# Scan layer of a two-layer block: operand offsets for GpSimd, VectorE's order over two units, and one PSUM bank moved

## The chip, the cores and the metric

The kernel runs on one core of a Trainium2 chip. A core has five engines that run side by side, each with its own in-order queue: TensorE (PE; its weight loads are listed as PEld), VectorE (DVE), ScalarE (ACT), GpSimd (POOL) and SyncE (SP), which here issues the DMAs. On-chip memory is SBUF, with 128 partitions, and PSUM, into which TensorE writes, used here as 8 banks of 512 float32 a partition. The metric is the device time of one execution in microseconds. Before the change, three runs gave a median of 8442.23 (8434.59 to 8457.52).

## The reference

The input is a 2 x 96 x 96 x 96 image batch (batch, channels, height, width). Layer 0 normalises over channels and goes through a 2-D selective scan; layer 1 is an attention layer; each is followed by a feed-forward block in a small float format. Only layer 0's scan changes. Cut to that:

```python
def selective_scan(u, delta, A, Bm, Cm, Dv):        # u: (windows, K=4, 192, L=36)
    def step(hst, inputs):
        ut, dt, bt, ct = inputs
        dA = jnp.exp(dt[..., None] * A)              # A: 16 states a channel
        hst = hst * dA + (dt * ut)[..., None] * bt[:, :, None, :]
        y = jnp.einsum('bkdn,bkn->bkd', hst, ct)
        return (hst, y)
    ...
    return jnp.moveaxis(ys, 0, -1) + Dv[None, :, :, None] * u
```

The image is cut into windows of 6 x 6 tokens, so a sequence has 36 tokens. Four directions are scanned: by rows, by columns, and both backwards. Ahead of the scan stand an input projection to 192 channels, a 3 x 3 convolution with GELU that gives an offset for every pixel, and a bilinear sampling at those offsets; behind it stand a layer norm, a gate and an output projection.

## The kernel before

**Staging.** Layer 0 works in 32 stripes (two images, 16 rows of windows); a stripe has T = 576 tokens. Three functions describe a stripe's work. `_l0_front` normalises, projects, convolves (`convolve`, L567), samples bilinearly on GpSimd (`sample`, L625 to L631) and makes the scan's inputs: the step sizes `dl` and the products `du` (the GpSimd lines L759 to L762 in `steps`), which go out to DRAM, and the B and C rows. `_l0_scan` runs the selective scan. `_l0_back` normalises, gates (L937) and projects its result and does the feed-forward block. While one stripe is scanned, the next one's front and the last one's back run between its instructions.

**The scan.** For each half of the channels, order and direction (`_l0_section`), four quarters `i` handle 4 of the 16 states each, and each quarter has two units `c` of 288 tokens: 64 units a stripe, 2048 in all. A partition is one (channel, state) pair, three channel blocks lie side by side, so an instruction works on 128 x 864 elements. A unit does this:

- `spread` (TensorE, L1056): copies the B row of its states to all partitions of the PSUM tile `bp`, a matmul with a 0/1 matrix;
- `product` (VectorE, L1060): multiplies `dur` with it and writes the product over all of `bp`, the last block first, so the B row is read before it is overwritten;
- `scan` (VectorE, L1076): runs h = h * dA + product along the tokens and writes `h` to SBUF;
- `times_c` (GpSimd, L1081): multiplies `h` in place by the C row, `cre`;
- `states` (TensorE, L1093): sums over states by matmul with `fold` into the PSUM tile `y`.

`decay` (ScalarE, L1041) makes `dA`, the exponentials, for both units of a quarter. SyncE loads `cre` for every quarter, `dlr` and `dur` for every section. There are six `h` buffers, two `dA`, two `bp`. The first unit's product also carries waits by hand (the `wait` call) for the decays of its quarter and for GpSimd and TensorE to be done with the `h` buffers that both units will use.

**PSUM.** `bp` has 2 buffers of 2 banks, `y` one bank, and the remaining 3 banks are the tag `p` (`P.np`), from which the front and the back take every matmul result: `pc` (convolution), `pb`, `pd`, `pt` (scan inputs), `yc`, `fxc` and so on.

**Offsets in SBUF.** A tile made with `skip=n` gets n unused elements (4 bytes each) at its front; `_place` cuts the view. Tiles are allocated at multiples of 32 bytes. `h` has a skip of 2, 4, 8 or 1 by quarter, with `lead=8` so that all have one size; `cre` has none. `dl`, `du`, `r`, `x1`, `x2`, `zs` and `fr` have different skips too.

**The order.** Nothing is issued directly. Each operation goes as an `_Op` with an engine, an estimated cost, the tiles it reads and writes, and a due time, to a planner (`_Plan`). `order()` is a list scheduler: it keeps a clock for each engine, adds a lag (`LAG`, by the engine that must wait) when the result comes from another engine, and picks the operation that can start first, with ties going to the earlier due time. Tiles take their buffers in the plan's order. The engines then run their instructions in exactly that order (`_in_order`); real waits are semaphores between them. A tile from `held` has no buffer and serves only to order operations. The unit's due times are `t0`, one `tau` = 3.4 us a unit.

Of the kernel before, what the change touches and what calls it, by code (L numbers as in the profile page):

```python
# [9 lines left out]
F32 = mybir.dt.float32  # L10
# [16 lines left out]
C = 96  # L27
HW = 96
# [62 lines left out]
class _Op:  # L91
    def __init__(self, eng, cost, run, due, tab):
        self.eng, self.cost, self.run, self.due, self.tab = eng, cost, run, due, tab
        self.deps, self.tiles, self.start, self.end = set(), [], None, None
        self.left, self.then, self.ready = 0, [], 0.0

SAME = 0.06  # L100
LAG = {"pe": 0.5, "dve": 1.5, "act": 0.6, "pool": 1.0, "sp": 1.5}


class _Plan:
# [6 lines left out]

    def tile(self, pool, shape, tag, bufs=1, dtype=F32, name=None, skip=None, lead=0):
        t = _Tile(self, pool, tag, bufs, shape, dtype, name or tag)
        t.skip, t.lead = skip, lead or skip
        return t
# [30 lines left out]
    def order(self):  # L146
# [13 lines left out]
        while len(out) < len(self.ops):  # L160
# [42 lines left out]
            for p in o.then:  # L203
                p.left -= 1
                p.ready = max(p.ready, o.end + (SAME if p.eng == o.eng else LAG[p.eng]))
                if not p.left:
                    ready[p.eng].append(p)
# [23 lines left out]
def _place(t, tag):  # L231

    if t.skip is None:
        return t.pool.tile(t.shape, t.dtype, tag=tag, name=t.name, bufs=1)
    n = math.prod(t.shape[1:])
    flat = t.pool.tile([t.shape[0], n + t.lead], t.dtype, tag=tag, name=t.name, bufs=1)
    v, d = flat[:, t.skip : t.skip + n], t.shape[1:]
    names = [f"d{j}" for j in range(len(d))]
    if len(d) == 1:
        return v  # L240
    return v.rearrange(f"p ({' '.join(names)}) -> p {' '.join(names)}", **dict(zip(names[1:], d[1:])))
# [200 lines left out]
def _cost(eng, cols):  # L442

    if eng == "pe":
        return 0.00175 * cols
    if eng == "act":
        return 0.2 + 0.0009 * cols
    if eng == "pool":
        return 0.1 + 0.00235 * cols
    return 0.08 + 0.00115 * cols  # L450
# [9 lines left out]
def _l0_front(k, P, S, f, x, b, s, at):  # L460
# [22 lines left out]
    def pool(cols, run, r, w):  # L483
        S.op("pool", _cost("pool", cols), run, r, w)


    xt, xin = temp([C, 8, HW], "xt"), S.tile(P.front, [C, 2, 8, HW + 2], "xin", 1)
    if lo > r0:
# [9 lines left out]
    )  # L498
    pool(8, lambda: nc.gpsimd.memset(xin.ap[:, :, :, 0 : HW + 2 : HW + 1], 0.0), (), (xin,))
    rows = lambda t, c: t.ap[:, 4 * c : 4 * c + 4, :].rearrange("p r w -> p (r w)")  # L500
# [26 lines left out]
    def project(half, c):  # L527
# [4 lines left out]
        act(N4, lambda: nc.scalar.copy(  # L532
            xin.ap[:, half, 4 * c : 4 * c + 4, 1 : HW + 1],
            pi.ap[:C, :N4].rearrange("p (r w) -> p r w", w=HW)), (pi,), ((xin, (half, c)),))
# [7 lines left out]

    zs = f.zs = S.tile(P.hand, [C, 2, T], "zs", 2, skip=12)

# [17 lines left out]
    def convolve(oh, c):  # L562
        pc = ps("pc")

        def part(ih, tap):
# [3 lines left out]
                k.w_c1[:, ih, tap, oh * C : (oh + 1) * C],  # L569
                xin.ap[:, ih, 3 * c + dy : 3 * c + dy + 3, dx : dx + HW],  # L570
                start=(ih == 0 and tap == 0),
# [16 lines left out]

    fr = temp([C, 2, WIN, HW], "fr", 5)

# [24 lines left out]
    xs1 = S.tile(P.front, [C, 2, T], "xs1", 1)  # L615
    dif, top, bot = temp([C, 2, 7, HW], "dif"), temp([C, 2, WIN, HW], "top", 2), temp([C, 2, WIN, HW], "bot")
    g = nc.gpsimd
    tt = g.tensor_tensor

    def sample(half):  # L620
        v = lambda: xin.ap[:, half, 1:8, 1 : HW + 1]
        fy, fx = lambda: fr.ap[:, 0], lambda: fr.ap[:, 1]
        d, tp, bt = (lambda u=u: u.ap[:, half] for u in (dif, top, bot))
        D, TP, BT = (dif, half), (top, half), (bot, half)
        pool(672, lambda: tt(d(), xin.ap[:, half, 1:8, 2 : HW + 2], v(), ALU.subtract), (xin,), (D,))  # L625
        pool(T, lambda: tt(tp(), d()[:, 0:6], fx(), ALU.mult), (D, (fr, 1)), (TP,))
# [35 lines left out]
    def order_of(o, xs):  # L662
# [50 lines left out]

        x1, x2 = row("x1", 1, skip=14), row("x2", 1, skip=9)

# [14 lines left out]
        def steps(m):  # L730
# [3 lines left out]
            u = x2 if m == 2 else x1  # L734
            e, du, r, w = (row(name, 2, skip=n) for name, n in (("e", 0), ("du", 1), ("r", 2), ("dl", 6)))
            for c in range(2):
# [271 lines left out]
def _l0_section(k, P, S, f, first, o, h, kk, py, at, tau):  # L1008
# [41 lines left out]
    def unit(u, i, c, cre, dA, t0):  # L1050
        toks = slice(c * H2, (c + 1) * H2)
        bp = S.tile(P.ps, [128, 1024], "bp", 2)
        ht = S.tile(P.rep, [128, NBL, H2], "h", P.nh, skip=(2, 4, 8, 1)[i], lead=8)

        def spread():
            nc.tensor.matmul(  # L1056
                bp.ap[:, :H2], k.selb[:, kk, i, :], f.bc[o].ap[:, toks], start=True, stop=True)

        def product():
            nc.vector.tensor_tensor(  # L1060
                bp.ap[:, : NBL * H2].rearrange("p (b n) -> p b n", b=NBL)[:, ::-1],
                dur.ap[:, ::-1, toks],
                bp.ap[:, :H2].unsqueeze(1).to_broadcast([128, NBL, H2]), ALU.mult)
            if c == 0:
                free = u + 1 - P.nh
                wait([("act", u), ("pool", free), ("pe", free)])

        S.op("pe", 0.3, spread, (f.bc[o],), (bp,), due=t0 - P.early["pe"] * tau)
        S.op("dve", 1.03, product, (dur,), (bp,), due=t0 - P.early["dve"] * tau)

        def scan():
            hv, dv = (v.rearrange("p b n -> p (b n)") for v in (ht.ap, dA.ap[:, c]))
            bv = bp.ap[:, : NBL * H2]
            if kk:
                hv, dv, bv = hv[:, ::-1], dv[:, ::-1], bv[:, ::-1]
            nc.vector.tensor_tensor_scan(hv, dv, bv, 0.0, ALU.mult, ALU.add)  # L1076

        S.op("dve", 2.0, scan, (dA, bp), (ht,), due=t0 + (1.35 - P.early["dve"]) * tau)

        def times_c():  # L1080
            nc.gpsimd.tensor_tensor(  # L1081
                ht.ap, ht.ap, cre.ap[:, toks].unsqueeze(1).to_broadcast([128, NBL, H2]), ALU.mult)
            P.issued["pool", u] = latest()

        S.op("pool", 2.06, times_c, (cre,), (ht,), due=t0 + (2.3 - P.early["pool"]) * tau)

        def states():
            end = o == 1 and kk == 1 and i == NQ - 1

            def part(dst, v, stop):  # L1090
                if o:
                    v = v.rearrange("p (w j i) -> p w i j", i=WIN, j=WIN)
                nc.tensor.matmul(dst, k.fold, v, start=False, stop=stop)  # L1093

            for blk in range(NBL):
                dst = py.ap[CB * blk : CB * blk + CB]
                n = HEAD - H2 if c else H2
                part(dst[:, c * H2 : c * H2 + n], ht.ap[:, blk, :n], end and c == 1)
            if c:
                for blk in range(NBL):  # L1100
                    part(_tail(py, blk), ht.ap[:, blk, n:], end and blk == NBL - 1)
            P.issued["pe", u] = latest()

        S.op("pe", 1.0, states, (ht,), (py,), due=t0 + (3.5 - P.early["pe"]) * tau)

# [4 lines left out]
def _layer0(k, tc, a, x, x2d):  # L1110
# [3 lines left out]
    with ExitStack() as st:  # L1114
# [12 lines left out]
        P.early = {"pe": 60, "act": 60, "dve": -30, "pool": 0, "sp": 8}  # L1127
        P.np, P.ng, P.nda, P.nh = 3, 5, 2, 6
        start = len(nc.cur_bb.bb.instructions)
        S, tau = _Plan(k), 3.4  # L1130
        stripes = [(b, s) for b in range(NB) for s in range(NW)]
        F = [Ctx() for _ in stripes]
# [834 lines left out]
```

## Time and profile before

| what | value |
|---|---|
| median of 3 runs | 8442.23 us |
| the profiled execution | 8449.37 us, span 8447.6 us |
| TensorE matmul busy in the span | 7320.6 us (87%) |
| VectorE busy | 7806.9 us (92%) |
| ScalarE busy | 6339.6 us (75%) |
| GpSimd busy | 5742.1 us (68%) |
| granted TensorE clock, mean | 0.907 |
| HBM traffic | 111 GB/s over the span |

The profile is of one execution. "Busy" is time in which at least one instruction of an engine ran; matmuls are pipelined, so a busy TensorE is not one at its peak. A line of the groups reads: source line, engine, operation, output <- inputs, shape, count | busy us, mean ns of one | idle time of the engine just before them and what ended most of it. A float32 matmul appears as two records. A line of a timeline reads: start, duration, engine, source line, operation, output <- inputs, shape, count; several equal ones in a row are merged into one.

### The profile page before, as it was taken

How to read it: one execution, taken by the hardware profiler on the slowest of the kernel's cores; microseconds unless marked ns; L12 is line 12 of the kernel's file. 1: busy time of each engine (PE TensorE's matmuls, PEld its weight loads, DVE VectorE, ACT ScalarE, POOL GpSimd, SP SyncE). 2: the span in 40 equal slices, each digit the busy share in tenths (PEclk: the TensorE clock that was granted, in tenths of full speed). 3: DMA queues.
4: the chain of work that ended last, by engine and by line, in shares of the span. 5: the costliest groups of instructions: out<-in, count | busy, mean ns of one | idle time of the engine just before them, and what ended most of it. 6: DMA issues, size and time to landing. Idle time of an engine off the chain costs nothing. (4 is left out here: it accounts for less than half of the span.)

```text
span 8447.6 us, 118902 instructions
## 1 busy us (share of the span) xinstructions
PE 7320.6 (87%) x43653; PEld 3406.4 (40%) x43653; DVE 7806.9 (92%) x5398; ACT 6339.6 (75%) x10688; POOL 5742.1 (68%) x3835
## 2 busy tenths in 40 slices
PE   7888888888888888888888888888857999989998
PEld 4444444444444444444444444444423223542245
DVE  3999999999999999999999999999996998959988
ACT  5777777777777777787777877787745886778867
POOL 4999989888889889999988999999873000110001
PEclk8898989999899889999989998999867999989999
DMA  2444444444444444444444444444442000110001
GB/s 89 142 153 152 152 154 150 149 153 146 148 151 149 149 148 153 155 151 150 155 152 147 149 153 150 152 154 155 147 135 63 3 2 14 36 48 3 2 22 33
DMA packets 339992, 985.62 MB, mean 117 GB/s; under 512 B 50152, under 2 KB 51872, under 8 KB 339104
## 3 DMA queue, kind: packets, MB, share of 16 engines
q1 hardware_dynamic: 337488, 977.74, 37.1%
q8 instruction: 347, 5.69, 0.3%
q14 instruction: 253, 2.07, 0.1%
q10 hardware_dynamic: 1904, 0.12, 0.0%
HBM read 797.19 MB, written 139.25 MB: 111 GB/s over the span
## 5 line engine op out<-in xcount | busy, mean ns | idle before, releaser
L1081 POOL TENSOR_TENSOR h<-h,cre 128x864 f32<-128x864 f32 x2048 | 3965.5, 1947 | 616.1 <-DVE h L1076 357.4
L1076 DVE TENSOR_TENSOR_SCAN h<-dA,bp 128x864 f32<-128x864 f32 x2048 | 3996.8, 1953 | 105.4 <-PE y L1093 27.2
L1041 ACT ACTIVATE dA<-dlr,A 128x576 f32<-128x576 f32 x3072 | 2156.5, 765 | 886.1 <-DVE h L1076 828.6
L1060 DVE TENSOR_TENSOR bp<-dur,bp 128x864 f32<-128x864 f32 x2048 | 2133.6, 1043 | 132.9 <-PE bp L1056 51.1
L1093 PE MATMUL y<-h,fold 128*32 128x288 f32 (+2 forms) x18432 | 1841.2, 446 | 154.4 <-POOL h L1081 152.6
L567 PE MATMUL pc<-xin,off 96*96 96x288 f32 x4608 | 1328.1, 420 | 0.0
L1056 PE MATMUL bp<-bt,selb 128*128 128x288 bf16 x2048 | 644.1, 316 | 700.4 <-DVE h L1076 683.7
L1429 ACT ACTIVATE pr<-sc 128x960 f32<-128x960 f32 (+1 forms) x1080 | 954.0, 937 | 202.8 <-PE sc L1425 182.5
L1093 PEld LDWEIGHTS y<-h,fold 128*32 128x32 f32 x18432 | 755.0, 117 | 857.6 <-issue 376.1
L1509 DVE TENSOR_TENSOR sums<-sums,pr 128x3840 f32<-128x3840 f32 (+1 forms) x240 | 959.0, 3996 | 56.9 <-ACT pr L1429 34.7
L567 PEld LDWEIGHTS pc<-xin,off 96*96 96x96 f32 x4608 | 705.2, 165 | 497.8 <-issue 247.2
L1601 POOL MEMSET vch<- 96x32 f32 x16 | 2.4, 152 | 1304.6 <-DVE dist L1463 1213.4
L1056 PEld LDWEIGHTS <-selb 128*128 128x128 bf16 x2048 | 201.5, 99 | 1455.9 <-DVE h L1076 1231.0
L1425 PE MATMUL sc<-qH,kH 32*128 32x480 f32 (+1 forms) x3240 | 627.2, 602 | 10.4 <-DMA q<-qH 5.6
L1425 PE MATMUL sc<-q,kH 32*128 32x480 f32 (+1 forms) x1080 | 564.7, 602 | 0.0
L1491 PE MATMUL av<-pr,vT 128*32 128x480 f32 (+1 forms) x4320 | 533.4, 564 | 3.6 <-ACT av L1516 3.5
L1682 DVE SCALAR_TENSOR_TENSOR acc<-vch,lepe_w,acc 96x1152 f32<-96x1152 f32 x320 | 469.0, 1466 | 7.9
L1425 PEld LDWEIGHTS sc<-qH,kH 32*128 32x128 f32 x3240 | 219.0, 184 | 419.7 <-issue 223.8
L883 POOL TENSOR_TENSOR x<-x,fy 96x576 f32<-96x576 f32 x32 | 53.3, 1664 | 479.1 <-ACT fy L882 415.1
L740 PE MATMUL pt<-xd,w_dt 96*128 96x288 f32 x768 | 304.1, 492 | 21.7 <-ACT xin L532 10.6
L761 POOL TENSOR_TENSOR dl<-dl,r 128x576 f32<-128x576 f32 x192 | 270.9, 1411 | 9.1 <-ACT dl L758 4.1
L762 POOL TENSOR_TENSOR du<-dl,x 128x576 f32<-128x576 f32 x192 | 271.7, 1415 | 6.6
(270 smaller groups left out, 9902.7 us busy)
## 6 DMA issues: line engine op xcount, KB each, us to landing
cre<-c_d SPq DMA_DIRECT2D x1024, 288.0 KB
dur<-du_d SPq DMA_DIRECT2D x256, 864.0 KB
dlr<-dl_d SPq DMA_DIRECT2D x256, 864.0 KB
x<-xs SPq DMA_DIRECT2D x512, 72.0 KB
du_d<-du SPq DMA_DIRECT2D x128, 288.0 KB
dl_d<-dl SPq DMA_DIRECT2D x128, 288.0 KB
du_d<-du SPq DMA_DIRECT2D x128, 144.0 KB
dl_d<-dl SPq DMA_DIRECT2D x128, 144.0 KB
```

The source lines that it names most:

```text
L567: pe(H2, lambda: nc.tensor.matmul(pc.ap[:C, :H2], k.w_c1[:, ih, tap, oh * C : (oh + 1) * C], xin.ap[:, ih, 3 * c + dy : 3 * c + dy + 3, dx ...
L1041: nc.scalar.activation(dA.ap[:, :, blk, :], dlr.ap[:, blk, :].rearrange("p (c n) -> p c n", c=2), AF.Exp, scale=k.A[:, i, kg, h, blk : blk ...
L1056: nc.tensor.matmul(bp.ap[:, :H2], k.selb[:, kk, i, :], f.bc[o].ap[:, toks], start=True, stop=True)
L1060: nc.vector.tensor_tensor(bp.ap[:, : NBL * H2].rearrange("p (b n) -> p b n", b=NBL)[:, ::-1], dur.ap[:, ::-1, toks], bp.ap[:, :H2].unsquee ...
L1076: nc.vector.tensor_tensor_scan(hv, dv, bv, 0.0, ALU.mult, ALU.add)
L1081: nc.gpsimd.tensor_tensor(ht.ap, ht.ap, cre.ap[:, toks].unsqueeze(1).to_broadcast([128, NBL, H2]), ALU.mult)
L1093: nc.tensor.matmul(dst, k.fold, v, start=False, stop=stop)
L1425: nc.tensor.matmul(two[to // 2][:, to % 2, :n], kH[rows, k0 : k0 + 128], q, start=True, stop=True)
L1429: nc.scalar.activation(pr[:, 2 * i : 2 * i + 2, :n], two[i][:, :, :n], AF.Exp, scale=HD**-0.5)
L1491: nc.tensor.matmul((main if s < HEADS else other)[s * HD : (s + 1) * HD, :n], vT[:, blk, hd, :], pr[:, place(s, p), :n], start=at == 0, st ...
L1509: nc.vector.tensor_tensor(both, both, pr[:, :, :, :n], ALU.add)
L1682: S.op("dve", 1.43, lambda: nc.vector.scalar_tensor_tensor(acc.ap, src(), W.lw[:, t : t + 1], acc.ap, ALU.mult, ALU.add), (vch,), (acc,))
```

## The change

Four edits of the scan's schedule and layout; the arithmetic is the same.

1. **Offsets.** `h` always has a skip of 2 elements, 8 bytes against `cre`; `du`, `r`, `x1`, `x2`, `zs` and `fr` get 2, `dl` gets 0, `top` 1. `xin` gets rows of 100 elements instead of 98 with the image at element 2. The parameter `lead` goes. The planner's cost of a GpSimd operation becomes 0.2 + 0.00177 us a column, and 1.75 for `times_c`.
2. **VectorE's order.** The two units of a quarter go as product, product, scan, scan. This is done with the held tile `turn`, which every product and scan writes, and by putting off the first unit's `rest()` until the second unit's product is planned.
3. **Banks.** The second unit's spread writes into a tile `B` of its own (one bank), and its product reads from there; the tag `p` gets 2 banks instead of 3.
4. **Lag.** For operations behind a spread the planner assumes 0.6 us on VectorE instead of 1.5 (`SOON`), since an `_Op` now carries its own lags.

```diff
+SOON = {"dve": 0.6}
...
-                p.ready = max(p.ready, o.end + (SAME if p.eng == o.eng else LAG[p.eng]))
+                p.ready = max(p.ready, o.end + (SAME if p.eng == o.eng else o.lag[p.eng]))
...
     if eng == "pool":
-        return 0.1 + 0.00235 * cols
+        return 0.2 + 0.00177 * cols
...
-    xt, xin = temp([C, 8, HW], "xt"), S.tile(P.front, [C, 2, 8, HW + 2], "xin", 1)
+    xt, xin = temp([C, 8, HW], "xt"), S.tile(P.front, [C, 2, 8, HW + 4], "xin", 1)
...
-    zs = f.zs = S.tile(P.hand, [C, 2, T], "zs", 2, skip=12)
+    zs = f.zs = S.tile(P.hand, [C, 2, T], "zs", 2, skip=2)
...
-    fr = temp([C, 2, WIN, HW], "fr", 5)
+    fr = temp([C, 2, WIN, HW], "fr", 2)
...
-        pool(672, lambda: tt(d(), xin.ap[:, half, 1:8, 2 : HW + 2], v(), ALU.subtract), (xin,), (D,))
+        pool(672, lambda: tt(d(), xin.ap[:, half, 1:8, 3 : HW + 3], v(), ALU.subtract), (xin,), (D,))
...
-        x1, x2 = row("x1", 1, skip=14), row("x2", 1, skip=9)
+        x1, x2 = row("x1", 1, skip=2), row("x2", 1, skip=2)
...
-            e, du, r, w = (row(name, 2, skip=n) for name, n in (("e", 0), ("du", 1), ("r", 2), ("dl", 6)))
+            e, du, r, w = (row(name, 2, skip=n) for name, n in (("e", 0), ("du", 2), ("r", 2), ("dl", 0)))
...
         bp = S.tile(P.ps, [128, 1024], "bp", 2)
-        ht = S.tile(P.rep, [128, NBL, H2], "h", P.nh, skip=(2, 4, 8, 1)[i], lead=8)
+        pB = S.tile(P.ps, [128, 512], "B", 1) if c else bp
+        ht = S.tile(P.rep, [128, NBL, H2], "h", P.nh, skip=2)
...
-                bp.ap[:, :H2].unsqueeze(1).to_broadcast([128, NBL, H2]), ALU.mult)
+                pB.ap[:, :H2].unsqueeze(1).to_broadcast([128, NBL, H2]), ALU.mult)
...
-        S.op("pe", 0.3, spread, (f.bc[o],), (bp,), due=t0 - P.early["pe"] * tau)
-        S.op("dve", 1.03, product, (dur,), (bp,), due=t0 - P.early["dve"] * tau)
+        S.op("pe", 0.3, spread, (f.bc[o],), (pB,), due=t0 - P.early["pe"] * tau).lag = SOON
+        S.op("dve", 1.0, product, (dur, pB) if c else (dur,), (bp, P.turn), due=t0 - P.early["dve"] * tau)
+
+        def rest():
+            def scan():
...
+            S.op("dve", 2.0, scan, (dA, bp), (ht, P.turn), due=t0 + (1.35 - P.early["dve"]) * tau)
...
-        S.op("pool", 2.06, times_c, (cre,), (ht,), due=t0 + (2.3 - P.early["pool"]) * tau)
+            S.op("pool", 1.75, times_c, (cre,), (ht,), due=t0 + (2.3 - P.early["pool"]) * tau)
...
+        if c == 0:
+            P.behind = rest
+        else:
+            P.behind()
+            rest()
...
-        P.np, P.ng, P.nda, P.nh = 3, 5, 2, 6
+        P.np, P.ng, P.nda, P.nh = 2, 5, 2, 6
...
+        P.turn, P.behind = S.held(k.ident, "turn"), None
```

## The prediction

> **What bounds the kernel now.** I read the busy times and the windows first, then the groups of instructions, then the timelines of single engines. The chain of waits follows the end of the run, which is layer 1, and says nothing of the part that changes. Two windows cut the run where the scan of layer 0 begins and ends (the columns are the window, its length, then busy time and instructions of PE, PEld, DVE, ACT, POOL, the granted clock, DMA share and GB/s):
>
> ```profile
> 145.00:6392.00 6247.00, 5292.92 (x31360) 2567.91 (x31358) 6051.30 (x4280) 4734.32 (x8163) 5575.11 (x3611) 0.89 0.48 149
> 6392.00:8447.00 2055.00, 1925.38 (x11979) 780.42 (x11976) 1739.72 (x1023) 1540.08 (x2401) 126.91 (x174) 0.96 0.08 21
> ```
>
> In the first, VectorE is busy 97% of the time, GpSimd 89%, TensorE 85%. So layer 0 runs at VectorE's pace, 6247 us for 32 stripes of 64 units, and the 2055 us of layer 1 stay. The groups say what VectorE does there and what it waits for:
>
> ```profile
> L1081 POOL TENSOR_TENSOR h<-h,cre 128x864 f32<-128x864 f32 x2048 | 3965.5, 1947 | 616.1 <-DVE h L1076 357.4
> L1076 DVE TENSOR_TENSOR_SCAN h<-dA,bp 128x864 f32<-128x864 f32 x2048 | 3996.8, 1953 | 105.4 <-PE y L1093 27.2
> ...
> L1060 DVE TENSOR_TENSOR bp<-dur,bp 128x864 f32<-128x864 f32 x2048 | 2133.6, 1043 | 132.9 <-PE bp L1056 51.1
> ```
>
> One product and one scan a unit, and little idle time: 132.9 us before products, of which 45.4 is the first load, and 105.4 before scans. The waits of this stretch name PE (51.1 and 28.8 before products, 27.2 before scans) and a handful of microseconds from others: some 124 us of stalls that a schedule could remove.
>
> **The order of VectorE.** VectorE's timeline (start, duration) has both orders in it, the old one nearly everywhere and the new one by chance a few dozen times:
>
> ```profile
> 4138.67 1.04 DVE L1060 TENSOR_TENSOR bp<-dur,bp 128x864 f32<-128x864 f32 x1
> 4139.74 1.95 DVE L1076 TENSOR_TENSOR_SCAN h<-dA,bp 128x864 f32<-128x864 f32 x1
> 4141.61 1.04 DVE L1060 TENSOR_TENSOR bp<-dur,bp 128x864 f32<-128x864 f32 x1
> 4142.69 1.95 DVE L1076 TENSOR_TENSOR_SCAN h<-dA,bp 128x864 f32<-128x864 f32 x1
> 4144.56 1.04 DVE L1060 TENSOR_TENSOR bp<-dur,bp 128x864 f32<-128x864 f32 x1
> ...
> 4150.45 2.00 DVE L1060 TENSOR_TENSOR bp<-dur,bp 128x864 f32<-128x864 f32 x2
> 4152.36 3.79 DVE L1076 TENSOR_TENSOR_SCAN h<-dA,bp 128x864 f32<-128x864 f32 x2
> 4156.07 1.04 DVE L1060 TENSOR_TENSOR bp<-dur,bp 128x864 f32<-128x864 f32 x1
> ```
>
> A scan that reads the product just before it starts 1.07 us after it, 0.03 after its end; an instruction that does not need its neighbour starts about 0.08 before the neighbour ends. Two units in the old order take 4144.56 - 4138.67 = 5.89 us; two in the new order 4156.07 - 4150.45 = 5.62 (others in the trace 5.64). So a pair gains 0.25 to 0.27. There are 1024 pairs, and in the records 1957 of the 2048 scans follow their product directly (elsewhere another instruction lies between and the gap is gone already): 0.956 x 1024 = 979 pairs, times 0.25 to 0.27, is 245 to 264 us. I take **-245**.
>
> The Trainium skill speaks against this: "VectorE: DVE Perf Modes", section "The DRAIN you can't avoid", measures a chain of copies as equally long with and without semaphores and says that such chaining gains nothing. By that sentence the reorder would be worth 0; the rows above disagree for a dependent pair, and the measured rows decide.
>
> **GpSimd's pairs.** GpSimd's timeline shows two prices for one shape:
>
> ```profile
> 3025.31 1.73 POOL L1081 TENSOR_TENSOR h<-h,cre 128x864 f32<-128x864 f32 x1
> ...
> 3028.52 1.71 POOL L1081 TENSOR_TENSOR h<-h,cre 128x864 f32<-128x864 f32 x1 [0.33 <-DVE h L1076]
> 3030.19 1.41 POOL L761 TENSOR_TENSOR dl<-dl,r 128x576 f32<-128x576 f32 x1
> 3031.91 2.03 POOL L1081 TENSOR_TENSOR h<-h,cre 128x864 f32<-128x864 f32 x1 [0.31 <-PE pt L740]
> ```
>
> Counted through the 2048 records, the first two of every eight take 1.71 us and the other six 2.02 (a quarter of one and three of the other give 1.945, the group's mean 1947). The first two are quarter i = 0, whose h lies 2 elements (8 bytes) off; the others lie 4, 8 and 1 off. The change puts all at 2: 1536 x 0.31 = 476 us less. `dl<-dl,r` and `du<-dl,x` (1.41 us, 4, 8 or 3 apart) should come to the 1.21 of `e<-e,du` and `r<-r,e`: 384 x 0.2 = 77. `Y<-Y,zs` adds 64 x 0.2 = 13. Together some 565 of GpSimd's 5575 us. The front's sampling (1.20 and 1.30) has no slow row to gain from; if `dif`, whose two reads stay one element apart, went to the slow rate, 64 x 0.2 = 13 us would come back.
>
> The skill's "GPSIMD Engine Reference", section 2.1, calls about 2.5 cycles an element a floor for two inputs; as an estimate that is 1.80 us for 864 elements at its 1.2 GHz, a gain of 0.22 a call instead of 0.31. The quarter at 1.71 is below it.
>
> None of this is on the path by itself: products and scans last 1.04 and 1.95 beside a busy or an idle GpSimd alike. Its worth is in the stalls. The stalls behind `y` (28.8 + 27.2) are TensorE's fold matmuls waiting for GpSimd, with the next spread behind them in TensorE's queue; part of the 51.1 is the same. Bounds 0 and -124; I take **-50**, near the 56 that the rows name. Without this cover the gain on VectorE would have met a GpSimd that needs 5575/32 = 174 us a stripe.
>
> **The spread and its bank.** The first unit's spread still writes into bp and needs the scan of the same slot. In the old order a scan and a product (2.95 us) lie between that scan's end and the product that needs the spread; in the new one a single scan, 1.87. The second unit's spread has a bank of its own, free as soon as the second product is done. But that product now stands ahead of the first scan: if its spread is late, both scans wait behind it. In the trace a free TensorE starts a spread 0.06 us after the scan's end and needs 0.30. Of 1024 first spreads, 101 start over 1.4 us after it, 85 us beyond in sum. So 0 to +85; since a stall once paid lets TensorE catch up, and part of the lateness is GpSimd's, I take **+30**.
>
> **TensorE's density.** Where the convolution runs, TensorE is full already:
>
> ```profile
> 2223.00:2295.00 72.00, 69.06 (x394) 33.80 (x386) 70.08 (x52) 53.64 (x85) 59.94 (x39) 0.89 0.48 149
> ```
>
> If VectorE is 4% faster (245 of 6247), these 72 us should be 69.1, all of which TensorE needs. If VectorE gets none of its gain here, 32 x 2.9 = +93; if the plan spreads the convolution, 0. I take **+45**.
>
> **Two banks for p.** I paired each p tile's first matmul with its last read: 11,997 us of holding in layer 0, 375 a stripe, 1.9 of 3 banks on average. Two banks over a stripe of 187 us offer 374. That would not do if holds were fixed, but much of them is queueing: `pb` is held 13.9 us for a few matmuls and copies of under 1 us, `pc` 19.2 for 36 matmul records of 0.29 (1328.1/4608), 10.4 of TensorE. Holds that shrink by a tenth suffice. From 0 to the third rival's price; I take **+10**.
>
> **What costs nothing.** No DMA is added, and SyncE's queue keeps its 1 load a quarter. The decays for quarter q+2 still wait for the second scan of q and have a pair's time, 5.62 in place of 5.89, for 3 x 0.70 us of ScalarE; without that slack each pair would lose what they overrun. The new costs and the shorter lag only move instructions. Layer 1 is planned with the new GpSimd cost, but has 126.91 us of GpSimd in 2055: 0 within 10.
>
> **Sum**: -245 - 50 + 30 + 45 + 10 = -210. The profiled execution took 8449.37 (span 8447.6), 7 above the median 8442.23, so 8239 there and **8232** against the median.
>
> **Rivals.**
> 1. The wait moves to the first spread: TensorE's queue is late for the shorter window. For it: 101 late spreads, the full stretch above, a granted clock of 0.70 in some windows. Against: the spread starts 0.06 us after its scan in most pairs. Price: +85 and +93 in full, nothing from GpSimd: 8442 - 245 + 178 = 8375.
> 2. Everything fits: stalls vanish with GpSimd's slack and pairs take 5.62: 8442 - 264 - 80 = 8098.
> 3. Slower: the two p banks set the pace. For it: 1.9 banks held on average. If holds stay at 375 us and each of 64 tiles a stripe loses 0.3 us at the hand-over between engines, a stripe takes (375 + 19)/2 = 197 us in place of 195.2, and the front's late work holds up spreads by the 85 above: 8442 + 58 + 85 = 8585. It decides once a stripe's holds pass 2 x 195 = 390 us.
> 4. The change does not do what it says: the next instruction still waits in the new order, as when two products in the trace were followed by a scan 2.5 us later. With some of GpSimd's relief against the tighter spread, 8440.
>
> **How the numbers follow.** Forecast 0.60, rival 1 0.16, rival 2 0.08, rival 3 0.12, rival 4 0.04. The forecast's own range is 8130 to 8340; reaching half into rivals 1 and 2 gives 8110 to 8430 with two tenths outside. This kernel's runs tell 0.3% (25 us) from no change: faster 0.83, same 0.04, slower 0.13.
>
> **What would show it.** The change's scans start about 0.96 after the second product and 1.86 after the first scan; `h<-h,cre` has a mean near 1715; `dl` and `du` near 1210; GpSimd's share in layer 0 falls to about 0.83; `PE y` vanishes among VectorE's waits while `PE bp` grows. It is wrong if products sit idle behind `PE bp` for over 200 us, or if matmuls of the front wait for ScalarE to empty a p bank.

## The result, and the profile after

The changed kernel takes **9131.14 us** (median of 4 runs, 9121.35 to 9136.23) against 8445.17 for the kernel before beside it: 1.0811 times as long, interval 1.0794 to 1.0828. It is slower by 686 us, where 210 less was forecast. The profiled execution took 9136.23 us, its span is 9134.4.

The same two windows as before, around the scan of layer 0 and after it (window, length, then busy time and instructions of PE, PEld, DVE, ACT, POOL, granted clock, DMA share, GB/s):

```profile
145.70:7082.20 6936.50, 5653.79 (x31374) 2760.20 (x31372) 5866.08 (x4280) 4831.68 (x8248) 5036.81 (x3609) 0.83 0.42 135
7082.20:9134.00 2051.80, 1926.66 (x11982) 780.48 (x11982) 1740.07 (x1023) 1541.09 (x2401) 127.29 (x175) 0.96 0.08 21
```

Layer 1 is as it was (2051.8 for 2055). Layer 0 went from 6247 to 6936.5 us, though VectorE's work in it shrank from 6051 to 5866 and GpSimd's from 5575 to 5037. VectorE is busy 85% of the time where it was busy 97%: the bound has become a wait. The groups name it:

```profile
L1079 DVE TENSOR_TENSOR_SCAN h<-dA,bp 128x864 f32<-128x864 f32 x2048 | 3884.6, 1937 | 926.8 <-PE y L1096 917.0
L1084 POOL TENSOR_TENSOR h<-h,cre 128x864 f32<-128x864 f32 x2048 | 3485.8, 1715 | 1796.7 <-DVE h L1079 858.3
...
L1062 DVE TENSOR_TENSOR bp<-dur,bp 128x864 f32<-128x864 f32 x1024 | 1068.4, 1043 | 150.2 <-ACT dA L1042 54.1
```

The scans sat idle 926.8 us, where they had been idle for 105.4; 917.0 of it ended when TensorE's matmuls into `y` (L1096, called the fold below) had read an `h` buffer. VectorE's stalls of over 0.1 us within layer 0, added up from its records, are 1070 us, before 132: 938 more. Layer 0 grew by 689, so the pairs did give back 249 us, about the 245 that the new order was to bring. The change did both things at once, and the loss is nearly four times the gain.

**Where the wait stands.** It comes at the same units of every stripe: in the mean of the 32 stripes 12.5 us in units 0 to 7, 5.8 in units 8 to 15 and 12.7 in units 32 to 39, of 33.4 in all. VectorE's timeline at the start of one stripe (start, duration; the bracket is the idle time before and its releaser):

```profile
2316.81 3.79 DVE L1079 TENSOR_TENSOR_SCAN h<-dA,bp 128x864 f32<-128x864 f32 x2
2320.52 1.04 DVE L1062 TENSOR_TENSOR bp<-dur,bp 128x864 f32<-128x864 f32 x1
2321.47 1.05 DVE L1062 TENSOR_TENSOR bp<-dur,B 128x864 f32<-128x864 f32 x1
2335.83 3.80 DVE L1079 TENSOR_TENSOR_SCAN h<-dA,bp 128x864 f32<-128x864 f32 x2 [13.32 <-PE y L1096]
2339.55 1.04 DVE L1062 TENSOR_TENSOR bp<-dur,bp 128x864 f32<-128x864 f32 x1
```

These are units 6 and 7 of the stripe: the six `h` buffers are full, and none comes free before TensorE has folded one. TensorE's timeline of the same time shows why it doesn't:

```profile
2322.70 4.06 PE L568 MATMUL pc<-xin,off 96*96 96x288 f32 x16
2326.60 0.28 PE L856 MATMUL fph<-fxq,f0w1q 96*128 96x288 fp8e5 x1
2326.73 3.08 PE L568 MATMUL pc<-xin,off 96*96 96x288 f32 x12
2329.65 0.28 PE L856 MATMUL fph<-fxq,f0w1q 96*128 96x288 fp8e5 x1
2329.77 3.57 PE L568 MATMUL pc<-xin,off 96*96 96x288 f32 x14
2333.18 1.13 PE L597 MATMUL po<-t,w_off 96*96 96x288 f32 x4
2334.24 0.61 PE L983 MATMUL y<-xs,w_D 96*32 96x504 f32 x1
...
2335.11 1.28 PE L1096 MATMUL y<-h,fold 128*32 128x288 f32 x22
```

`direct` (L983) opens the `y` bank of the new half and must come before every fold. It stands in TensorE's fixed order behind the next stripe's convolution (L568), which at this point should have been done. The windows of eight units of the stripe from 2303.66 show that, counting the convolution alone (window, length, busy time and instructions of PE and PEld, granted clock, DMA share, GB/s):

```profile
2303.66:2339.55 35.89, 25.71 (x99) 15.37 (x98) 1.00 0.37 111
2339.55:2368.72 29.17, 0.00 (x0) 0.00 (x0) 0.66 0.36 111
2368.72:2391.85 23.13, 0.00 (x0) 0.00 (x0) 0.99 0.53 169
2391.85:2414.34 22.49, 0.00 (x0) 0.00 (x0) 0.91 0.38 122
2414.34:2454.11 39.77, 0.00 (x0) 0.00 (x0) 0.66 0.48 147
2454.11:2479.24 25.13, 0.00 (x0) 0.00 (x0) 0.58 0.31 102
2479.24:2503.12 23.88, 0.00 (x0) 0.00 (x0) 0.80 0.43 151
2503.12:2525.96 22.84, 13.45 (x46) 6.79 (x46) 1.00 0.47 153
```

The fourth window, 22.49 us for four pairs, is the pace that the order was to bring (5.62 a pair). The convolution begins in the last eight units of the stripe and spills into the first eight of the next, where TensorE is full and VectorE waits. In the kernel before it lay in the last 24 units and was over in time. The last three windows of a stripe there, cut and counted in the same way:

```profile
2238.88:2264.14 25.26, 17.90 (x51) 9.20 (x52) 0.80 0.47 145
2264.14:2287.71 23.57, 14.19 (x51) 7.14 (x49) 1.00 0.50 154
2287.71:2311.28 23.57, 12.31 (x45) 6.69 (x44) 1.00 0.41 125
```

So the front is late, and the front's matmul results all go through the p banks.

**What holds the p banks.** Pairing each p tile's first matmul with its last read, as for the prediction: a stripe held banks for some 375 us before and some 363 now; three banks were all in use about 30% of the time before, and the two are both in use about 70% of the time now. One holder stands out. The back needs its `yc` tiles two at a time: the copy out of the first overwrites `Y`, which the second one's matmul still reads, so the first keeps its bank until the second has one too. TensorE's timeline of one stripe, two `yc` tiles of a pair and the tiles between:

```profile
2360.29 1.28 PE L909 MATMUL yc<-Y,less_mean 96*96 96x288 f32 x2 [0.82 <-ACT xs L648]
2361.36 1.17 PE L909 MATMUL yc<-Y,minus_mean 96*96 96x288 f32 x2
2364.39 1.28 PE L640 MATMUL px<-top,ident 96*96 96x288 f32 x2
...
2408.39 0.73 PE L909 MATMUL yc<-Y,minus_mean 96*96 96x288 f32 x2 [0.86 <-ACT r L747]
2408.95 0.65 PE L909 MATMUL yc<-Y,less_mean 96*96 96x288 f32 x2
```

From 2360.3 to 2413.6 one of two banks is held by half a pair, and everything between goes through the other one. The mean hold of a `yc` tile is 17.5 us (longest 56.7), before 6.1 (longest some 17).

### The profile page after: what moved, and what is told of

Same layout as the page of the kernel before. It is cut to its first block, busy times and chain, and to the rows that moved or that the text cites. A ratio compares the mean times of both kernels' runs of the same rounds, so it can differ in the third digit from the quotient of the medians.

```text
span 9134.4 us, 119246 instructions
## 1 busy us (share of the span) xinstructions
PE 7685.6 (84%) x43653; PEld 3596.2 (39%) x43653; DVE 7622.0 (83%) x5398; ACT 6434.5 (70%) x10768; POOL 5203.6 (57%) x3835
## 5 line engine op out<-in xcount | busy, mean ns | idle before, releaser
L1079 DVE TENSOR_TENSOR_SCAN h<-dA,bp 128x864 f32<-128x864 f32 x2048 | 3884.6, 1937 | 926.8 <-PE y L1096 917.0
L1084 POOL TENSOR_TENSOR h<-h,cre 128x864 f32<-128x864 f32 x2048 | 3485.8, 1715 | 1796.7 <-DVE h L1079 858.3
L1096 PE MATMUL y<-h,fold 128*32 128x288 f32 (+2 forms) x18432 | 1838.3, 455 | 292.0 <-POOL h L1084 287.8
L568 PE MATMUL pc<-xin,off 96*96 96x288 f32 x4608 | 1253.4, 409 | 13.5 <-ACT fh L859 7.0
L1096 PEld LDWEIGHTS y<-h,fold 128*32 128x32 f32 x18432 | 793.1, 121 | 1157.0 <-POOL h L1084 698.6
L1062 DVE TENSOR_TENSOR bp<-dur,bp 128x864 f32<-128x864 f32 x1024 | 1068.4, 1043 | 150.2 <-ACT dA L1042 54.1
L1062 DVE TENSOR_TENSOR bp<-dur,B 128x864 f32<-128x864 f32 x1024 | 1076.0, 1051 | 0.0
L568 PEld LDWEIGHTS pc<-xin,off 96*96 96x96 f32 x4608 | 711.2, 162 | 404.3 <-issue 62.7
L1058 PE MATMUL B<-bt,selb 128*128 128x288 bf16 x1024 | 339.6, 332 | 282.5 <-DVE bp L1062 277.9
L1058 PE MATMUL bp<-bt,selb 128*128 128x288 bf16 x1024 | 337.5, 330 | 282.2 <-DVE h L1079 275.7
L741 PE MATMUL pt<-xd,w_dt 96*128 96x288 f32 x768 | 354.4, 560 | 110.7 <-DVE xn L525 53.9
L746 ACT ACTIVATE e<-pt,dt_b 128x288 f32<-128x288 f32 x384 | 189.9, 495 | 199.7 <-PE pt L741 198.1
```

Source lines behind the costliest of these rows:

```text
L568: pe(H2, lambda: nc.tensor.matmul(pc.ap[:C, :H2], k.w_c1[:, ih, tap, oh * C : (oh + 1) * C], xin.ap[:, ih, 3 * c + dy : 3 * c + dy + 3, dx ...
L1058: nc.tensor.matmul(pB.ap[:, :H2], k.selb[:, kk, i, :], f.bc[o].ap[:, toks], start=True, stop=True)
L1062: nc.vector.tensor_tensor(bp.ap[:, : NBL * H2].rearrange("p (b n) -> p b n", b=NBL)[:, ::-1], dur.ap[:, ::-1, toks], pB.ap[:, :H2].unsquee ...
L1084: nc.gpsimd.tensor_tensor(ht.ap, ht.ap, cre.ap[:, toks].unsqueeze(1).to_broadcast([128, NBL, H2]), ALU.mult)
```

## The experiments

Two theories stood at the start. BANKS: two p banks starve the front, which makes TensorE late for `y`. ORDER: the new order of VectorE is itself to blame, by the shorter time that it leaves the first spread. Each time below is a median of 4 runs (e4: 10), each ratio against the kernel before on the same chip.

**The parts, one at a time.** e1 is the kernel before with one digit changed:

```diff
-        P.np, P.ng, P.nda, P.nh = 3, 5, 2, 6
+        P.np, P.ng, P.nda, P.nh = 2, 5, 2, 6
```

> The kernel before with the tag p cut from 3 banks to 2 and nothing else: VectorE's order, offsets, spread and lags stay. Theory BANKS (two p banks cannot carry the front and the back of a stripe in a stripe's scan time, so the front falls behind and the scan waits for what it queues on TensorE): 8950 to 9250 us, with VectorE's scans idle behind y matmuls for 600 us or more. Theory ORDER (the strict order product, product, scan, scan with the tighter first spread makes the stalls): 8445 within 60, since the order is the old one.

Measured: 9245.73 us, 1.0948 (1.0927 to 1.0969). Taking one bank away costs 800 us, with no other edit. The wait is that of the kernel after (VectorE's waits: line, what it waited for: us in total, times, longest):

```profile
DVE h L1076 <- PE y L1093: 725.1, 98, 17.7
```

BANKS holds here.

e2 is the kernel after with the bank split undone:

```diff
-        pB = S.tile(P.ps, [128, 512], "B", 1) if c else bp
+        pB = bp
...
-        ... product, (dur, pB) if c else (dur,), (bp, P.turn), ...
+        ... product, (dur,), (bp, P.turn), ...
...
-        P.np, P.ng, P.nda, P.nh = 2, 5, 2, 6
+        P.np, P.ng, P.nda, P.nh = 3, 5, 2, 6
```

> The changed kernel with the bank move undone: the second unit's spread goes back into its own bp and p has 3 banks; order, offsets and lags as changed. BANKS: the stalls behind y vanish and the order's gain shows, less some idle time before the second product, whose spread must now wait for the second scan: 8200 to 8400 us. ORDER: stays at 9000 or more.

Measured: 8600.27 us, 1.0176 (1.0157 to 1.0194), 531 less than the kernel after. ORDER falls, but BANKS' range, 8200 to 8400, is missed by 200 us. No scan waits for `y` any more. Another wait has come, and VectorE's waits name it:

```profile
DVE bp L1062 <- PE bp L1058: 507.9, 504, 4.6
```

The second unit's spread now has to wait for the second scan, with one product between that scan and its own. So the two bank layouts fail in two ways: two p banks make scans wait for `y`, three make products wait for their spread.

e3 is the kernel after with only the order undone (`rest()` called at once for both units):

> The changed kernel with only VectorE's order undone (product, scan, product, scan; B, two p banks, offsets and lags as changed). BANKS: still clearly slower than before, 8600 to 9300 us, with scans waiting for y. ORDER: back to 8400 to 8450 us.

Measured: 8847.11 us, 1.0477 (1.0458 to 1.0495); scans wait 426.2 us for `PE y`. Most of the loss is there without the new order, and the new order adds 284 to it. That a faster VectorE only reaches the late front sooner would fit; no run shows it by itself.

e4 is the kernel before with the new offsets alone (`skip=2` for `h`, and so on), planned with the old costs, so that the order is that of before:

> The kernel before with the new offsets alone (h, du, dl, x1, x2, zs, fr, top and xin); the planner's costs are the old ones, so every engine has the order of before. h<-h,cre at 1715 ns throughout, dl and du at 1210. If GpSimd's lateness made the stalls of before (124 us), 8350 to 8400 us; if GpSimd is off the path, 8445 within 15.

Measured: 8439.63 us, 0.9988 (0.9978 to 0.9997). The group `h<-h,cre` falls to 1715 ns, GpSimd's work in layer 0 from 5575 to 5025 us, and the time by 6.6: 550 us taken off an engine that nobody waits for long. Of the 56.0 us that VectorE waited for `PE y` before, 41.3 are left (24.9 and 16.4).

**What starves the front.** e5 lets `direct` and the copy of `y` come ahead of the convolution:

```diff
-        S.op("pe", 1.4, direct, (f.xs0,), (py,), due=t0)
+        S.op("pe", 1.4, direct, (f.xs0,), (py,), due=t0 - 200 * tau)
...
-        S.op("act", 1.4, out, (py,), (f.Y,), due=t0 + 33 * tau)
+        S.op("act", 1.4, out, (py,), (f.Y,), due=t0 - 167 * tau)
```

> The kernel after, with one thing altered: `direct` (TensorE's D*x into the y bank) and `out` (ScalarE's copy of the y bank) are due 200 tau and 167 tau before the half begins, so that convolution can no longer win the tie against them. STARVE (the long waits of scans for `PE y` come from `direct` being ordered behind convolution at the switch of the half, and the banks are a bystander): the scan's 917 us behind `PE y` fall below 300 and the time to 8350-8600. BANKS (the front and back run late because two p banks can't hold their tiles, and VectorE waits for that work in the end, wherever it stands): the time stays within 100 us of 9131, and the stall moves to other units or other waits of VectorE, whose sum over 0.1 us each stays above 850 us (1070 in the kernel after).

Measured: 9215.53 us, 1.0912 (1.0894 to 1.0930). STARVE falls. 760.6 us of the waits for `y` are left, 257.2 have become waits of the back's own instruction on VectorE (`Y`, L929, behind `yva`), and the stalls add up to 1151 us. The place of the wait was a symptom: with it moved, the sum of the stalls did not fall.

e6 keeps the pair of `yc` tiles together:

```diff
-        o.due = at(sofar / whole)
+        o.due = at(sofar / whole) - (2000.0 if getattr(o, "rush", False) else 0.0)
...
                    "yc", ((Y, c),)) for h in range(2)]
+        S.ops[-1].rush = True
+        S.ops[-1].deps.add(S.ops[-2])
+        if c:
+            S.ops[-2].deps.add(P.yc)
+        P.yc = S.ops[-1]
```

> The kernel after, with one thing altered in the order: the second of the two `yc` matmuls that the back needs as a pair is put directly behind the first one (due 2000 us early, and a pair begins only when the pair before it has both), so that no bank is held by one half of a pair while its partner waits for a bank. Banks, copies and all arithmetic are the same. PAIR (part of what two banks cost is that a `yc` tile holds one of the two for up to 57 us, mean 17.5 against 6.1 us before, while its partner queues behind the front's tiles): mean hold of yc falls to 5-8 us, the waits of scans for `PE y` by a third or more, and the time by 200-500 us, to 8630-8930. COUNT (it is only that 363 us of holds per stripe don't fit into two banks, whoever holds them): less than 80 us, 9050-9140.

Measured: 8819.34 us, 1.0439 (1.0422 to 1.0456): 312 us less, from an edit that touches the order alone. TensorE's timeline of the pair that had lain 48 us apart:

```profile
2264.70 1.27 PE L909 MATMUL yc<-Y,less_mean 96*96 96x288 f32 x2 [0.67 <-ACT xs L648]
2265.77 1.17 PE L909 MATMUL yc<-Y,minus_mean 96*96 96x288 f32 x2
...
2269.24 1.28 PE L909 MATMUL yc<-Y,minus_mean 96*96 96x288 f32 x2
2270.31 1.17 PE L909 MATMUL yc<-Y,less_mean 96*96 96x288 f32 x2
```

The mean hold of `yc` is 5.6 us, and the stall in units 32 to 39, 12.7 us in the mean of the kernel after's stripes, is 2.7. PAIR holds for this plan. The 13.3 us at the start of the stripe stay; the convolution is still late.

e7 takes the fourth edit of the change back, the shorter planning lag, which the prediction had put at nothing:

```diff
-        ... spread, (f.bc[o],), (pB,), due=t0 - P.early["pe"] * tau).lag = SOON
+        ... spread, (f.bc[o],), (pB,), due=t0 - P.early["pe"] * tau)
```

> The kernel after without its shorter planning lag for spreads (the spread is planned with the same lag as before behind VectorE, so it is ordered a little later on TensorE). BANKS: the lag is no part of the loss, the time stays at 9050-9200, with the same waits for `PE y`. LAG (a spread that is planned too early is put ahead of other matmuls and its wait for VectorE holds up TensorE's queue, and with it the convolution and `direct`): TensorE's queue waits less for VectorE, the scan's waits for `PE y` fall by half, and the time falls to 8500-8800.

Measured: 8627.50 us, 1.0212 (1.0195 to 1.0229): 504 us less than the kernel after. LAG's numbers hold: scans wait 181.2 us for `y`, the convolution begins eight units earlier in the stripe, and spreads at the head of TensorE's queue wait 283 us for VectorE (154.1 and 128.5) where they waited 554 (275.7 and 277.9). The reason that LAG gives, that such waits hold up TensorE's queue, is not shown, for they come to 684 us in the kernel before and to 674 in e8, the fastest run below. The other side of it is products behind `PE bp`, 247.5 us against 15.7. The mean `yc` hold is 7.7 us: this plan splits a pair in one stripe only, so e6 and e7 may partly mend the same thing.

e12 is the same edit on e2, three p banks:

> e2 (three p banks, the second spread in its own product tile) without the short planning lag; with the kernel after, e2 and e7 it fills a table of two by two. LAG ALONE (the short lag is a loss in itself, some 500 us as between the kernel after and e7): 8050-8250. WITH TWO BANKS ONLY (the short lag is harmful where two banks starve the front, and useful where the second spread waits for a scan, since without it the plan leaves VectorE idle between a spread and its product): 8700-9100, slower than e2.

Measured: 9127.58 us, 1.0817 (1.0793 to 1.0841), 527 us more than e2, 28 above the range of WITH TWO BANKS ONLY, whose direction holds; LAG ALONE falls. VectorE's timeline under the convolution shows the price, both products of each pair late:

```profile
2503.26 1.06 DVE L1062 TENSOR_TENSOR bp<-dur,bp 128x864 f32<-128x864 f32 x1 [0.76 <-PE bp L1058]
2504.75 1.06 DVE L1062 TENSOR_TENSOR bp<-dur,bp 128x864 f32<-128x864 f32 x1 [0.43 <-PE bp L1058]
2505.72 3.79 DVE L1079 TENSOR_TENSOR_SCAN h<-dA,bp 128x864 f32<-128x864 f32 x2
2510.26 1.06 DVE L1062 TENSOR_TENSOR bp<-dur,bp 128x864 f32<-128x864 f32 x1 [0.74 <-PE bp L1058]
```

926.8 us of products behind `PE bp`. The table that the four make (us, medians):

| | short lag | old lag |
|---|---|---|
| two p banks, spread's own bank | 9131.14 (after) | 8627.50 (e7) |
| three p banks, spread in bp | 8600.27 (e2) | 9127.58 (e12) |

No row and no column is the better one: moving the bank costs 531 us under the short lag and gains 500 under the old one. Lag and banks act through one plan, and their effects don't add.

**With measured numbers in the plan.** The planner's costs were off from the trace on both sides: product 1.0 us against 0.95 from start to start, scan 2.0 against 1.85, a hand-over to TensorE 0.5 against 0.06. e8 is e2 with these corrected:

```diff
-SOON = {"dve": 0.6}
-LAG = {"pe": 0.5, "dve": 1.5, "act": 0.6, "pool": 1.0, "sp": 1.5}
+SOON = {"dve": 0.1}
+LAG = {"pe": 0.05, "dve": 1.5, "act": 0.6, "pool": 1.0, "sp": 1.5}
...
-        return 0.2 + 0.0009 * cols
+        return 0.2 + 0.0006 * cols
...
-        S.op("dve", 1.0, product, ...
+        S.op("dve", 0.92, product, ...
-            S.op("dve", 2.0, scan, ...
+            S.op("dve", 1.85, scan, ...
...
-                t0, t1 = (64 * n - 90) * tau, (64 * n - 12) * tau
+                t0, t1 = (64 * n - 95) * tau, (64 * n - 5) * tau
```

together with `direct` and `out` due 20 tau earlier. ScalarE's cost, the front's window (its last edit above) and the due times change too, and no run tells these edits apart.

> A version meant to keep what the change gained: the kernel after, with three p banks and the second unit's spread in its own product tile as in e2, and with the planner told the durations that the traces show (product 0.92 for 1.0, scan 1.85 for 2.0, ScalarE 0.0006 us a column for 0.0009, TensorE's lag 0.05 for 0.5 and behind VectorE 0.1 for 0.6), `direct` and `out` due 20 tau earlier, and the front's window 12 tau longer (95 to 5 tau ahead for 90 to 12). ORDER (the new order of VectorE is worth its 0.25 us on each of 979 pairs once the front gets its banks and the plan its true costs): 6247 us of the scan's layer before become 5950-6050, the time 8130-8260, faster than before by 2 to 4%. WAIT (what held e2 back is the second product's wait for the second scan's bank, 508 us, which no cost of the planner alters): that wait stays above 350 us and the time at 8450-8600.

Measured: **8251.53 us**, 0.9769 (0.9753 to 0.9786). It beats both kernels. Layer 0 takes 6054 us, 4 above the range. VectorE's stalls there are 184 us, mostly one line:

```profile
DVE bp L1062 <- PE bp L1058: 149.6, 191, 3.5
```

WAIT falls: of the 508 us of e2 the plan's edits took 358, with the layout as it was. The convolution's windows, eight units each, in a stripe of e8 (its last four shown; columns as above):

```profile
2161.89:2184.73 22.84, 11.36 (x39) 5.67 (x38) 1.00 0.42 136
2184.73:2207.56 22.83, 12.92 (x43) 6.21 (x42) 1.00 0.45 153
2207.56:2230.03 22.47, 12.46 (x42) 6.22 (x42) 1.00 0.51 160
2230.03:2252.49 22.46, 5.65 (x19) 2.63 (x18) 1.00 0.48 155
```

It lies over some 32 units and ends before the stripe does. The windows under it are 22.46 to 22.84 us long, against 22.47 for four pairs at full pace, so it costs VectorE next to nothing.

e9 is e8 with the bank split put back as in the kernel after, and nothing else altered:

> e8 with one thing altered back: the front's and back's tiles have two p banks and the second unit's spread its own bank, as in the kernel after; VectorE's order, the offsets, the planner's durations, lags, windows and due times are e8's. BANKS (two p banks cannot carry the front at the pace of the new order, whatever the plan is told): the time is 8700-9000, 450-750 us above e8, with VectorE waiting for `PE y` again. PLAN (with true durations two banks suffice, and the change lost only because its plan rested on wrong costs): 8200-8400, and the product's 150 us of waits for `PE bp` in e8 vanish as the second spread has its own bank.

Measured: 9104.80 us, 1.0781 (1.0763 to 1.0799): 853 us more than e8, above the range on BANKS' side. VectorE's waits:

```profile
DVE xn L525 <- ACT ava L522: 532.8, 58, 68.5
DVE h L1079 <- PE y L1096: 444.4, 65, 16.6
```

Within layer 0 the first line comes to 439.6 us, so over two fifths of its 1030 us of stalls are now for the front's own layer norm. In the trace its tiles come only after a `yc` tile has held its bank for some 50 us of the stripe. That this hold is the cause is shown in part: with the pairs kept together (e13 below) 298.8 us of the 532.8 are left. PLAN falls: measured numbers don't make two banks enough.

e10 is e8 with VectorE's old order. It differs from e8 in one thing more, which its expectation overlooks: its spreads are planned with the old lag of 1.5 us, e8's with 0.1:

> e8 with VectorE's order undone: the kernel before (product, scan, product, scan; three p banks; the spread in its own product tile) with the new offsets on GpSimd and with the same durations, lags, windows and due times in its plan as e8. ORDER (e8's gain is the order: 0.25 us on 979 pairs, about 245 us): 8380-8480, no better than the kernel before by more than 60 us and 130-240 us above e8. PLAN (e8's gain is the better plan and the order brings nothing): 8240-8300, as e8.

Measured: 8359.25 us, 0.9893 (0.9877 to 0.9910), between the two ranges. Of e8's gain of 190 us, the better plan and the offsets give 82 to 89 (by the two sets of runs of the kernel before), and the order and the short lag together 108. That the 108 are the order's alone is not shown, since no run parts the two. The order's full worth is 245 by the spacing of instructions, and the stalls account for the rest: 184 us in e8 and 46 in e10, so 138 are given back, 133 of them to late spreads (149.6 against 16.5).

e11 is e9 with the old lag:

> e9 with one thing altered: the planning lag from a spread to VectorE is the old 1.5 us, not the short one. If the short lag and two banks hurt each other as e7 showed (9131 became 8627 without it), this gains 300 us or more on e9, to 8400-8600, but stays above e8 by more than 150 us, since the holds of the p tiles are what they were. If e7's gain came of the plan's wrong durations alone, it makes no difference to e9 here (within 60 us).

Measured: 8698.37 us, 1.0281 (1.0253 to 1.0308): 406 us less than e9, 98 above the range's end. The short lag harms two banks under these costs too. The split pair is still there, though, about 44 us long in 29 of the stripes; one of them on TensorE:

```profile
2237.99 0.73 PE L909 MATMUL yc<-Y,less_mean 96*96 96x288 f32 x2 [1.57 <-ACT Y L921]
...
2280.98 0.65 PE L909 MATMUL yc<-Y,minus_mean 96*96 96x288 f32 x2
```

e13 is e9 with the pairs kept together as in e6, and e14 is e13 with the old lag:

> e9 with the edit of e6 (the two `yc` matmuls of a pair one behind the other, so that neither holds a bank while the other waits for one). PAIR (in e9 one bank is held 53 us of each stripe of 218 by half a pair, and VectorE stalls 27.6 us in the units that follow): that stall falls below 8 us, yc's mean hold from 16.5 to 5-7 us, the time by 300-650 us, to 8450-8800. SHORTAGE (the holds don't fit into two banks anyway, the stall only moves): less than 150 us, 8950-9105.

> e13 with the old planning lag of 1.5 us from a spread to VectorE. SHORTAGE REMAINS (even with no split pair two banks are more than 100 us slower than e8's three): 8350-8650. ALL PAIR (with pairs together two banks do as well as three): 8200-8350, within 100 us of e8.

Measured: e13 8806.01 us, 1.0427 (1.0410 to 1.0444); e14 8693.34, 1.0296 (1.0279 to 1.0313). The pair is worth 299 us on this plan, a hair under the range; the mean `yc` hold is 6.6 us, and the stall in units 32 to 39 goes from 25.3 to 14.8 in the mean of the stripes, not below 8. With the old lag, keeping pairs together is worth 5 us (e14 against e11), which is within the spread of e11's runs, though e14 has no hold of a `yc` tile over 12 us where e11 had 44 in nearly every stripe. So a split pair does not cost by being split alone; it cost 300 us in two plans and nothing in a third. e14 misses its range by 43, on the side of SHORTAGE: with no pair split, two banks are still 442 us behind e8's three (which have the short lag). The best run with two p banks is e7's 8627.50.

## Why the prediction was wrong, point by point

- **The order of VectorE, -245: right.** In the trace after, product to product is 0.949 us from start to start, product to scan 0.961, scan to scan 1.864, scan to product 1.844 (medians), together 5.618; before 1.076 and 1.870 twice, 5.892. What was got in the kernel after, 249 us, is the difference of stalls and length. "VectorE: DVE Perf Modes", section "The DRAIN you can't avoid", has a chain of copies take as long with semaphores as without. That does not carry over to a dependent neighbour here: a scan that needs the product before it starts 1.076 us after it, one that doesn't 0.961, so the dependence adds 0.115.
- **GpSimd, -50: the price was right, the worth was not.** 565 us of GpSimd's time were forecast and 538 came (1715 ns for `h<-h,cre`, 1206 for `dl` and `du`). Alone it is worth 6.6 us (e4). The stalls behind `y`, which the term was to remove, were mostly not GpSimd's: 41.3 of 56.0 us are left with GpSimd 550 us lighter. The sampling did have slow rows: `top<-top,xin` and `bot<-bot,xin` went from 1.30 to 1.20 us, and `dif` stayed at 1.30.
- **First spread, +30: not seen in this kernel.** Products wait 15.7 us for `PE bp`, where they waited 51.1. That wait was forecast to grow and fell, in a kernel whose VectorE stands still for `y` instead. It grows to 508 where the second spread has no bank of its own (e2), and to 247.5 with one of its own and the old lag (e7).
- **TensorE's density, +45: the place was right, the cause another.** The convolution is where VectorE loses time in the kernel after, but because it starts late. Where the plan spreads it (e8), the windows under it lose 0 to 0.4 us each, near the lower bound of 0.
- **Two banks for p, +10: the step that failed.** "Holds that shrink by a tenth suffice" treated bank time as something to be poured from one stripe into a tank of 2 x 187 us. The holds shrank by 3%, not by a tenth, since a bank is also held while its tile waits for another bank: half a pair of `yc` waited 53 us. Taking the bank away measured +800 (e1); moving it to the second spread +531 (e2 to after) and +853 (e8 to e9). It is no fixed price: under the old lag and the old costs the move gains 500 (e12 to e7). Rival 3 named the banks and the late front, but had it hold up spreads, and mis-sized it at 143 us; the trace has 917.0 us behind `y` and 15.7 behind spreads. Its "It decides once a stripe's holds pass 2 x 195 = 390 us" is wrong as well, since two banks decided at some 363, and in e13 at some 311, with both in use only 54% of the time. The mean of the holds says nothing of which tiles must be held at once.
- **"The new costs and the shorter lag only move instructions": the second failure.** The lag alone is 504 us in this kernel (e7), and 527 the other way with three banks (e12). In a kernel whose whole order comes from a planner, a number of the planner is a change of the program.
- **The signs.** Of the two signs of being wrong, the first, products idle behind `PE bp` for over 200 us, did not come (15.7). The second, matmuls of the front that wait for a p bank to be emptied, did, for the front's tiles and the back's, in small waits of TensorE about once a stripe each. In the following waits the instruction named makes no input of the matmul but is the last to read another p tile, and so frees its bank:

```profile
PE pt L741 <- DVE xn L525: 53.9, 29, 2.0
PE px L640 <- ACT xs L648: 25.1, 30, 0.9
PE yc L909 <- ACT r L747: 24.0, 30, 0.9
PE yc L909 <- ACT xs L648: 23.2, 29, 0.8
PE pt L741 <- ACT zs L551: 23.2, 27, 1.3
```

  In all, TensorE's idle time before matmuls into p tiles within layer 0 is 382 us, 86 in the kernel before and 84 in e8; waits for inputs are in it too. The sum is well under VectorE's 938 more, and the code says why: the planner knows of the full banks and puts other matmuls in between. So most of the shortage shows as front work that is late a whole window later, under the name of `y`. And `PE y` did not vanish, it became the bound.

What stays open: why exactly the short lag costs 504 us with two banks and gains 527 with three, why a split pair costs 300 us in two plans and nothing in e11's, and what sets the remaining 442 us of e14. The runs show the effects and their sizes, not that chain of choices in the plan.

## What to carry to other kernels

Count buffers by what their users need at the same moment, and by what a holder waits for, not by the mean of their occupancy: a mean of 1.9 of 3 said that two would nearly do, and in the kernel after a pair needed at once kept one of the two from all other use for a quarter of the stripe. When an edit gives a resource to one side, price the side that loses it by taking it away alone: one digit told 800 us. And where an order is planned, put measured durations into the plan before judging a layout by it; the same three-bank layout took 8600 and 8252 us, with measured costs and shifted due times between the two.

## What the runs showed of the hardware

The granted clock of TensorE differed between the runs: 0.907 over the whole run before, 0.855 after, 0.927 in e8, 0.944 in e10. It did not simply follow VectorE's stalls, since e8 has 184 us of them and the kernel before 132. In the kernel after's windows above it was 1.00 under the convolution, stall or not, and 0.58 to 0.66 in three of the windows with or next to a stall and without convolution. There the four matmul records of a `pd` took 2.23 us (at 2426.35) that had taken 1.16 (at 2372.77, in a window at 0.99). So a late front may be made later: while TensorE has little to do, the little that it does goes slower. No run here set this apart. "TensorE: Matmul & The Clock Gate", section "What's actually happening", says that activity releases a throttle and idleness puts it back; the windows agree in direction.

GpSimd's price by operand offset held in every run that has it: 1.715 us for `h<-h,cre` with `h` 8 bytes off `cre`, 2.02 at the other offsets of the kernel before.
